# A graph layer on one core: half-block counts in PSUM, earlier loads in the head, and three blocks of the next chunk ahead of a fetch

## The chip, the cores and the metric

The kernel runs on one core of a Trainium2 chip. The metric is the time of one execution on the device, in microseconds (us), as a median over several executions. The profile shows one execution of the program with the busy times of five engines: TensorE (PE; its weight loads are PEld), VectorE (DVE), ScalarE (ACT), GpSimd (POOL) and SyncE (SP, which here only issues DMAs).

## The reference

The program computes one layer of a graph network. There are 12,500 nodes with 64 features each and 212,500 edges, sorted by their destination `dst`. For each edge, two rows of the normalised nodes and one edge weight go through a two-layer network with 128 hidden features; the results are summed per node `src`, which is not sorted; and a node network uses the sums.

```
h   = relu(layernorm(x))
e   = silu(concat(h[src], h[dst], edge_weight1) @ eW1 + eb1)
e   = silu(e @ eW2 + eb2)
agg = segment_sum(e, src)
out = x + silu(concat(h, agg) @ nW1 + nb1) @ nW2 + nb2
```

## The kernel before

**Tables.** The first matrix product is split. Table `ta` holds `h @ eW1` for the `src` half (three bf16 parts), table `tb` that for the `dst` half. `feed` is the generator that makes these tables from `x`, a few steps at a time, beside other work (`groups`, `products`, `normed`). A small table `tb0` for the first 2048 nodes is made at the very start (`first_rows`), so that the first `EARLY` blocks need not wait for `tb`.

**Buckets.** The 12,500 nodes are spread over `NB` = 100 buckets of 125. Edges are handled in the order given, in blocks of `BLK` = 1024, and each edge is sent to a row of its own in the DRAM array `q` of its bucket. There are 208 blocks, divided into 11 chunks: chunk 0 has 8 blocks, the ten others 20 (the last one slightly fewer). Each chunk has its own `q`.

**The sending side, per block s.**
- `load` (L256 on) issues on SP: the lists `bc` and `bb` of one block ahead (L265, L267), and two windows of the `tb` table, `win` (L277).
- `count` has three parts. First `pick` and `oh` (L302, L303), masks of which window row and which bucket an edge has; then the edge weights are loaded into `pick` (L288) and a scan counts each edge's place in its bucket (L306); then `own` keeps the count of the edge's own bucket (L314).

```
nc.vector.tensor_tensor_scan(
    run, oh, nil.to_broadcast([NB, BLK]), carry.get(c, -1.0), op0=OP.add, op1=OP.add
)
```

`run` (100 x 1024, fp32) lies in SBUF, and `nil`, one zero per partition, in the PSUM tile `misc`. `carry` is the last count of the block before.
- `send` has three parts: eight small matmuls write the places into `rank`, a part of `misc` (L333); sixteen matmuls give the row `qp` of each edge (L341), copied to `qs` (L348), and VectorE computes the destination `to` (L353); then GpSimd issues one indirect DMA for each 128 edges (L362), eight for a block. There are eight `qs` buffers of four such DMAs each, and four `to` buffers.

`send_all(c)` runs through the blocks of a chunk and yields after each part: `PIECES` = 3 pieces for a block, `send(s)` together with `count(s + 1)`. It also issues, on ACT's queue, the zero fills of the next chunk's `q`.

**The receiving side.** A chunk is processed in 25 batches of four buckets; a batch takes one step in chunk 0 and two in the others, 525 steps in all. `fetch` (L407, L412) loads a batch's `q` rows and `ta` rows on SP, `NQ` = 4 batches ahead. A step goes through `s_lr` (L430), `s_one_t` (L435), `s_pt` (L444, L451), `s_one` (L464), `s_p2` (L483), `s_seg` (sums per node into the PSUM tile `seg`, L497) and `s_add` (adds `seg` to `aggT` in SBUF, L508). In the last chunk each batch is followed by the node network (`nodes`).

**The order.** TensorE, VectorE, ScalarE and SyncE run in the order written by hand[...]. In the head, the lists are prepared and all of chunk 0 is sent, with four steps of `feed` after each piece. Then chunk 0's first four batches are fetched. From there the list `turn` gives the order within a step, with four hooks (`None`), at which pieces of the next chunk are sent and `feed` goes on:

```
turn = [
    (s_pt, 1), (s_add, -2), (s_one_t, 2), None, (s_bias, 1), (s_p2, 0), (s_one, 0), None, (s_seg, -1), None, (s_lr, 3), None,
]
```

How many pieces are due at a hook follows from `marks`: chunk c has to be sent completely before its first fetch is issued, and pieces are spread evenly between two such points.

[...] Before, `mm` takes four, `p2` two, `misc` one and `seg` one.

Of the kernel before, what the change touches and what calls it, by code (L numbers as in the profile page):

```python
# [28 lines left out]
F32 = mybir.dt.float32  # L29
# [4 lines left out]
OP = mybir.AluOpType  # L34
# [4 lines left out]
P = 128  # L39
L = 125  # L40
WL = 48
HB = 64
BLK = 1024
HALF = BLK // 2
TB = BLK // P
PAIR = 2 * BLK
G = 4
# [12 lines left out]
def tile_gnn(ctx: ExitStack, tc: tile.TileContext, x, src, dst, ew, eW1, eb1, eW2, eb2, nW1, nb1, nW2, nb2, out):  # L60
    nc = tc.nc
# [43 lines left out]
            dma(to[part], of[part])  # L105

    CH = 12
    NE, EARLY = 16, 24
    x_rows = x.rearrange("(l b) d -> l b d", b=NB)

    ident = const.tile([P, P], F32, name="ident")
# [127 lines left out]
    with ExitStack() as work:  # L239
# [5 lines left out]
                engines={mybir.EngineType.PE, mybir.EngineType.DVE, mybir.EngineType.Activation, mybir.EngineType.SP}  # L245
            )
        )
        misc = sgp.tile([P, 4 * TB], F32, name="misc")
        nc.vector.memset(misc[:, 2 * TB : 2 * TB + 1], 0.0)
        nil = misc[:NB, 2 * TB : 2 * TB + 1]  # L250
        oh = cnt.tile([NB, BLK], F16, name="oh")
        run = cnt.tile([NB, BLK], F32, name="run")
        carry = {}
        blk = {}
        nblocks = -(-E // BLK)
        chunk_of = [c for c, ch in enumerate(chunks) for _ in range(2 * (ch[1] - ch[0]))][:nblocks]  # L256

        def load(s, ahead=0):

            if s + ahead < nblocks:  # L260
                p, g = (s + ahead) // 2, (s + ahead) % 2
# [6 lines left out]
                blk[s + ahead] = [bc, bb]  # L268
            if 0 <= s < nblocks:
# [26 lines left out]
        def count(s):  # L296

            if s >= nblocks:
                return
            c = chunk_of[s]  # L300
            bc, bb, win, pick = blk[s]
            nc.vector.tensor_scalar(pick, bc, same, plus, op0=OP.is_equal, op1=OP.add)  # L302
            nc.vector.tensor_scalar(oh, bb[:NB, :], part[:NB, :], None, op0=OP.is_equal)  # L303
            yield
            weights(s)
            nc.vector.tensor_tensor_scan(  # L306
                run, oh, nil.to_broadcast([NB, BLK]), carry.get(c, -1.0), op0=OP.add, op1=OP.add
            )
            yield
            n = min(BLK, E - s * BLK)  # L310
            end = run[:, n - 1 : n]
            carry[c] = end
            own = wk.tile([NB, BLK], F16, name="own")
            nc.vector.tensor_tensor(own, run, oh, op=OP.mult)  # L314
            blk[s].append(own)
            if s + 1 == nblocks or chunk_of[s + 1] != c:
                u = wk.tile([NB, 1], F32, name="u")
                for limit, op in ((chunks[c][2] * P - 1, OP.is_gt), (chunks[c][3] - 1, OP.is_lt)):
                    nc.vector.tensor_scalar(u, end, float(limit), None, op0=op)
                    nc.vector.tensor_tensor(bad[:NB, 1:2], bad[:NB, 1:2], u, op=OP.add)  # L320
            yield

        def send(s):

            p, g = s // 2, s % 2
            c = chunk_of[s]
            _, _, cap, _, q = chunks[c]
            _, _, win, pick, run = blk.pop(s)
            n = min(BLK, E - s * BLK)
            nt = -(-n // P)  # L330
            rank = misc[:, (s % 2) * TB : (s % 2 + 1) * TB]
            for t in range(nt):
                nc.tensor.matmul(rank[:, t : t + 1], run[:, t * P : (t + 1) * P], fours[:NB, :], start=True, stop=True)  # L333
            yield

            qps = [mm.tile([P, G, H], F32, name="qp", tag="mm") for _ in range(2)]
            for t in range(G):
                for a in range(2):
                    half = slice(a * HB, a * HB + WL + 2)
                    if a * G + t < nt:  # L340
                        nc.tensor.matmul(  # L341
                            qps[a][:, t, :], pick[half, t * P : (t + 1) * P], win[half, :], start=True, stop=True
                        )
            halves = []
            for t0 in range(0, nt, G):
                qs = qsp.tile([P, G, W], F32, name="qs")
                m = min(G, nt - t0)
                nc.scalar.copy(qs[:, :m, :H], qps[t0 // G][:, :m, :])  # L348
                halves.append((t0, m, qs))
            for t0, m, qs in halves:  # L350
                if t0 == 0:
                    to = top.tile([P, TB], I32, name="to")
                    nc.vector.scalar_tensor_tensor(  # L353
                        to[:, :nt], rank[:, :nt], float(G * cap * P), bkE[:, g * TB : g * TB + nt, p], op0=OP.min, op1=OP.add
                    )
                at = g * TB + t0
                nc.scalar.copy(
                    qs[:, :m, H:], locE[:, at : at + m, p][:, :, None].to_broadcast([P, m, W - H])
                )
                for t in range(t0, t0 + m):  # L360
                    k = min(P, n - t * P)
                    i = nc.gpsimd.indirect_dma_start(  # L362
                        out=q[:],
                        out_offset=bass.IndirectOffsetOnAxis(ap=to[:k, t : t + 1], axis=0),
                        in_=qs[:k, t - t0, :],
                        in_offset=None,
                    )

                    tc.declare_no_dep(i.ins, group=f"rows{c}", reason="each edge has a row of its own")
                    tc.add_to_no_dep_group(f"rows{c}", i.ins)  # L370
                yield

        def send_all(c):
# [2 lines left out]
            zeros_left = list(fill(c + 1, nc.scalar, 7)) if c + 1 < len(chunks) else []  # L376
            each = -(-len(zeros_left) // len(mine))
            for s in mine:
                load(s + 2, 1)
                for f in zeros_left[:each]:  # L380
                    f()
                del zeros_left[:each]
# [14 lines left out]
        def fetch(i):  # L397
# [17 lines left out]
            batch[c, B] = [qt, a3, None]  # L415
            if c == len(chunks) - 1:
                node_in[B] = nodes_in(B, ndp[0])

# [3 lines left out]
            return batch[c, B], [((g * G + t) % n * G + (g * G + t) // n, (g * G + t) // n) for t in range(G)]  # L422

        def s_lr(k):
            (qt, _, _), tiles = of(k)
# [11 lines left out]

        def s_pt(k):

            (qt, a3, _), tiles = of(k)  # L440
# [15 lines left out]
            st[k]["e1"] = e1  # L456

        def s_one(k):
            (qt, _, _), tiles = of(k)
# [29 lines left out]

        def s_seg(k):  # L490
            c, B, n, g = steps[k]
            item, tiles = of(k)
            if g == 0:
                item[2] = sgp.tile([P, G, L], F32, name="seg")
            e2, one = st[k].pop("e2"), st[k].pop("one")
            for t, (j, b) in enumerate(tiles):
                nc.tensor.matmul(item[2][:, b, :], e2[:, t, :], one[:, t, :], start=j < G, stop=j >= G * (n - 1))  # L497

        def s_add(k):
            c, B, n, g = steps[k]  # L500
            if g < n - 1:
                return
            v = aggT[:, B * G : B * G + G, :]
            seg = batch.pop((c, B))[2]
            if c == 0:
                nc.vector.tensor_copy(v, seg)  # L506
            else:
# [192 lines left out]
        with tc.tile_pool(name="lists", bufs=1, side="right") as lp:  # L700
# [18 lines left out]
            for _ in turns(steps_, 3):  # L719
                if zero_fills:  # L720
                    zero_fills.pop(0)()
            for _ in turns([by_edges(sf, bkE)] + [first_rows(g) for g in range(0, NE, G)], 3):
                pass
            scale(0)
            load(-1, 1)
            load(0, 1)
            load(1, 1)
            for _ in by_edges(t, locE):
                pass
            for _ in count(0):  # L730
# [13 lines left out]
            nc.scalar.copy(b2f, p2)  # L744
        ld2 = work.enter_context(tc.tile_pool(name="ld2", bufs=NQ))
        ndp = []
        for i in range(NQ):
            fetch(i)


        first = -3
        marks, total = [(0, 0)], 0
        for c in range(1, len(chunks)):
            start = c * (NB // G) - NQ
            by = sum(x[2] for x in batches[: start + 1]) - 2
            total += PIECES * pending[c]
            marks.append((hooks * (by - first), total))
        pieces = itertools.chain.from_iterable(send_all(c) for c in range(1, len(chunks)))
        at = done = 0
        for k in range(first, len(steps) + 2):  # L760
            for s in turn:
                if s is None:
# [170 lines left out]
```

## Time and profile before

| | |
|---|---|
| median of 3 runs | 2703.32 us (2700.62 to 2704.18) |
| profiled execution: time | 2702.45 us |
| profiled execution: span | 2700.7 us |
| TensorE busy | 2188.2 us (81%) |
| VectorE busy | 1874.6 us (69%) |
| ScalarE busy | 1251.1 us (46%) |
| GpSimd busy | 1818.5 us (67%) |
| indirect DMAs (L362) | 1661, mean 1072 ns |
| scans (L306) | 208, mean 2341 ns (2278 in the 11 without a carry) |
| own (L314) | 208, mean 1220 ns |

A row of the profile names the line, the engine, the operation, and what it writes and reads; "idle before" is the time for which the engine did nothing just ahead of an instruction, with what released it. "issue" stands for time in which the engine waited for nothing that the profile shows. In the strip of slices each digit is the busy share of a fortieth of the span, in tenths.

### The profile page before, as it was taken

How to read it: one execution, taken by the hardware profiler on the slowest of the kernel's cores; microseconds unless marked ns; L12 is line 12 of the kernel's file. 1: busy time of each engine (PE TensorE's matmuls, PEld its weight loads, DVE VectorE, ACT ScalarE, POOL GpSimd, SP SyncE). 2: the span in 40 equal slices, each digit the busy share in tenths (PEclk: the TensorE clock that was granted, in tenths of full speed). 3: DMA queues.
4: the chain of work that ended last, by engine and by line, in shares of the span. 5: the costliest groups of instructions: out<-in, count | busy, mean ns of one | idle time of the engine just before them, and what ended most of it. 6: DMA issues, size and time to landing. Idle time of an engine off the chain costs nothing.

```text
span 2700.7 us, 59194 instructions
## 1 busy us (share of the span) xinstructions
PE 2188.2 (81%) x21814; PEld 2043.3 (76%) x21814; DVE 1874.6 (69%) x2634; ACT 1251.1 (46%) x2689; POOL 1818.5 (67%) x1728
## 2 busy tenths in 40 slices
PE   2436674898699599699879969959959987997997
PEld 1326574897699599599779869959958986996996
DVE  4736683796588488588768858848857885883443
ACT  2325551454355255355445535525535544553443
POOL 2546787777777777777777777777777777773000
PEclk9757786998899799799989989979989998998999
DMA  8668675876776777686787777767767755764441
GB/s 201 190 186 243 202 246 163 260 234 196 231 234 229 213 248 236 203 251 231 212 256 230 237 218 233 238 205 253 231 202 250 240 183 198 234 199 158 158 164 52
DMA packets 257969, 577.18 MB, mean 214 GB/s; under 512 B 51201, under 2 KB 110579, under 8 KB 257468
## 3 DMA queue, kind: packets, MB, share of 16 engines
q1 hardware_dynamic: 185096, 384.91, 44.3%
q0 software_dynamic: 54144, 123.04, 12.6%
q10 hardware_dynamic: 18434, 65.37, 10.5%
q8 instruction: 175, 2.87, 0.4%
q14 instruction: 120, 0.98, 0.1%
HBM read 361.44 MB, written 211.67 MB: 212 GB/s over the span
## 4 chain that ended last, share of the span: by engine, by line
PE 63%; DMA 13%; issue 6%; POOL 5%; DVE 2%; ACT 1%; SPq 0%; DVEq 0%; POOLq 0%; ACTq 0%
PE p L483 15%; PE seg L497 15%; PE pt L451 11%; DMA q<-qs,to 8%; PE pt L444 8%; PE qp L341 7%; POOL q L362 5%; PE lr L430 4%; DMA pick<-in_edge_weight_dram 3%; PE misc L333 1%; DMA bb<-rows 1%; PE z L216 1%; PE o L225 1%; DVE oneT L435 1%; PE z L219 1%
## 5 line engine op out<-in xcount | busy, mean ns | idle before, releaser
L362 POOL DMA_INDIRECT q<-qs,to x1661 | 1780.4, 1072 | 632.2 <-issue 445.6
L455 ACT ACTIVATE e<-pt 128x512 f32<-128x512 f32 x525 | 313.9, 598 | 778.0 <-PE pt L451 765.1
L483 PE MATMUL p<-w,e 128*128 128x128 f32 x4200 | 588.2, 284 | 2.2 <-ACT p L477 2.2
L497 PE MATMUL seg<-one,e 128*128 128x125 f32 x4200 | 576.8, 281 | 8.9 <-DVE aggT L506 5.7
L483 PEld LDWEIGHTS p<-w,e 128*128 128x128 f32 x4200 | 529.5, 198 | 27.5 <-issue 10.4
L497 PEld LDWEIGHTS seg<-one,e 128*128 128x128 f32 x4200 | 524.8, 196 | 11.2 <-ACT p L477 4.1
L435 DVE TENSOR_SCALAR oneT<-lr,part 125x512 bf16<-125x512 f32 x525 | 392.6, 748 | 197.5 <-PE lr L430 194.6
L306 DVE TENSOR_TENSOR_SCAN run<-oh,run,misc 100x1024 f32<-100x1024 f16 x197 | 461.1, 2341 | 1.0 <-PE misc L333 0.7
L451 PE MATMUL pt<-oneT,a 125*128 125x256 bf16 (+1 forms) x3300 | 444.6, 274 | 0.0
L341 PE MATMUL qp<-win,pick 50*128 50x128 f32 x3322 | 264.6, 300 | 205.0 <-DMA pick<-in_edge_weight_dram 119.9
L348 ACT COPY qs<-qp 128x512 f32<-128x512 f32 x416 | 224.7, 588 | 444.3 <-PE qp L341 312.0
L341 PEld LDWEIGHTS qp<-win,pick 50*128 50x128 f32 x3322 | 224.1, 202 | 237.8 <-issue 208.2
L444 PE MATMUL pt<-ident,qt 128*128 128x128 f32 x2100 | 332.8, 282 | 68.8 <-DVE oneT L435 68.8
L508 DVE TENSOR_TENSOR aggT<-aggT,seg 128x500 f32<-128x500 f32 x250 | 168.3, 673 | 315.7 <-PE seg L497 313.3
L464 DVE TENSOR_TENSOR one<-nodes,qt 128x500 f32<-128x500 f32 x525 | 353.4, 673 | 0.5 <-PE seg L497 0.5
L451 PEld LDWEIGHTS <-a 125*128 125x128 bf16 x3300 | 320.5, 100 | 34.5
L487 ACT ACTIVATE e<-p 128x512 f32<-128x512 f32 x525 | 314.6, 599 | 12.3 <-PE p L483 11.6
L477 ACT COPY p<-b2f 128x512 f32<-128x512 f32 x525 | 312.3, 595 | 0.1
L444 PEld LDWEIGHTS pt<-ident,qt 128*128 128x128 f32 x2100 | 228.4, 145 | 74.9 <-DVE oneT L435 72.9
L430 PE MATMUL lr<-identb,qt 128*125 128x128 bf16 x2100 | 215.1, 226 | 63.1 <-DMA qt<-q 63.0
L314 DVE TENSOR_TENSOR own<-run,oh 100x1024 f16<-100x1024 f32 x208 | 253.7, 1220 | 0.0
L430 PEld LDWEIGHTS <-qt 128*125 128x125 bf16 x2100 | 187.8, 140 | 75.6 <-DMA qt<-q 63.7
(122 smaller groups left out, 1094.5 us busy)
## 6 DMA issues: line engine op xcount, KB each, us to landing
qt<-q SPq DMA_DIRECT2D x250, 576.0 KB
a<-ta SPq DMA_DIRECT2D x275, 384.0 KB
q<-zeros ACTq DMA_DIRECT2D x30, 1638.0 KB
bb<-rows SPq DMA_DIRECT2D x208, 224.0 KB
bc<-rows SPq DMA_DIRECT2D x208, 128.0 KB
q<-qs,to POOLq DMA_INDIRECT x1661
win<-tb SPq DMA_DIRECT2D x416, 24.0 KB
ta<-parts SPq DMA_DIRECT2D x25, 384.0 KB
```

The lines of the kernel that those rows point to most:

```text
L306: nc.vector.tensor_tensor_scan(run, oh, nil.to_broadcast([NB, BLK]), carry.get(c, -1.0), op0=OP.add, op1=OP.add)
L341: nc.tensor.matmul(qps[a][:, t, :], pick[half, t * P : (t + 1) * P], win[half, :], start=True, stop=True)
L362: i = nc.gpsimd.indirect_dma_start(out=q[:], out_offset=bass.IndirectOffsetOnAxis(ap=to[:k, t : t + 1], axis=0), in_=qs[:k, t - t0, :], in ...
L430: nc.tensor.matmul(lr[:L, t, :], loc[:, at : at + 1].to_broadcast([P, L]), identb, start=True, stop=True)
L435: nc.vector.tensor_scalar(oneT, st[k].pop("lr")[:L], part1[:L, :], None, op0=OP.is_equal)
L444: nc.tensor.matmul(pt[:, t, :], qt[:, j, :H], ident, is_transpose=True, start=t == 0, stop=False, skip_group_check=True)
L451: nc.tensor.matmul(pt[:, cols, :], a3[:L, b, i, :], oneT[:, cols, :], start=False, stop=i == 2, skip_group_check=True)
L455: nc.scalar.activation(e1, pt, AF.Silu)
L464: nc.vector.tensor_tensor(one.rearrange("p (b j) l -> p b j l", j=n), nodes1[:, None, None, :].to_broadcast(wide), loc[:, tiles[0][1] : ti ...
L483: nc.tensor.matmul(p2[:, t, :], e1[:, t, :], w2, start=False, stop=t == G - 1, skip_group_check=True)
L487: nc.scalar.activation(e2, p2, AF.Silu)
L497: nc.tensor.matmul(item[2][:, b, :], e2[:, t, :], one[:, t, :], start=j < G, stop=j >= G * (n - 1))
```

## The change

Three things change together.

The counts: `run` is now one PSUM tile of 512 columns, and a block is scanned in two halves, each followed by its half of `own`. The second half's scan starts from the last count of the first. The first half stands in the second part of `count`, the other one in the third. `nil` becomes a tile in SBUF. So that `run` has a bank, `seg` and `rank` now share the tile `misc`[...], and `rank` has one buffer instead of two.

The head: the lists of block 0 are loaded (`load_rows(0)`) before `first_rows` issues its stores to `tb0`, and `scale(0)`, four short VectorE instructions, runs inside that loop.

The chunks: after the head's sending of chunk 0, three blocks (`LEAD` = 9 pieces) of chunk 1 are sent, again with four steps of `feed` after each piece, and only then come the first fetches. `marks` keep this distance up to the last chunk but one. `EARLY` grows from 24 to 30 blocks.

```
-    NE, EARLY = 16, 24
+    NE, EARLY = 16, 30
...
-        misc = sgp.tile([P, 4 * TB], F32, name="misc")
-        nc.vector.memset(misc[:, 2 * TB : 2 * TB + 1], 0.0)
-        nil = misc[:NB, 2 * TB : 2 * TB + 1]
+        misc = sgp.tile([P, G * L + TB], F32, name="misc")
+        seg = misc[:, : G * L].rearrange("p (b l) -> p b l", l=L)
+        rank = misc[:, G * L :]
+        run = sgp.tile([NB, HALF], F32, name="run")
         oh = cnt.tile([NB, BLK], F16, name="oh")
-        run = cnt.tile([NB, BLK], F32, name="run")
+        nil = cnt.tile([NB, 1], F32, name="nil")
+        nc.vector.memset(nil, 0.0)
...
-            nc.vector.tensor_tensor_scan(
-                run, oh, nil.to_broadcast([NB, BLK]), carry.get(c, -1.0), op0=OP.add, op1=OP.add
-            )
-            yield
-            n = min(BLK, E - s * BLK)
-            end = run[:, n - 1 : n]
-            carry[c] = end
             own = wk.tile([NB, BLK], F16, name="own")
-            nc.vector.tensor_tensor(own, run, oh, op=OP.mult)
             blk[s].append(own)
+            for h in range(2):
+                half = slice(h * HALF, (h + 1) * HALF)
+                n = min(HALF, E - s * BLK - h * HALF)
+                if n <= 0:
+                    break
+                nc.vector.tensor_tensor_scan(
+                    run, oh[:, half], nil.to_broadcast([NB, HALF]), carry.get(c, -1.0), op0=OP.add, op1=OP.add
+                )
+                end = carry[c] = run[:, n - 1 : n]
+                nc.vector.tensor_tensor(own[:, half], run, oh[:, half], op=OP.mult)
+                if h == 0:
+                    yield
...
-            rank = misc[:, (s % 2) * TB : (s % 2 + 1) * TB]
...
-            for _ in turns([by_edges(sf, bkE)] + [first_rows(g) for g in range(0, NE, G)], 3):
-                pass
-            scale(0)
-            load(-1, 1)
-            load(0, 1)
-            load(1, 1)
+            load_rows(0)
+            counting = count(0)
+            for i, _ in enumerate(turns([by_edges(sf, bkE)] + [first_rows(g) for g in range(0, NE, G)], 3)):
+                if i == 8:
+                    scale(0)
+            for i in range(2):
+                load(i)
...
+        LEAD = 3 * PIECES
+        for done in range(1, LEAD + 1):
+            next(pieces)
+            for _ in range(4):
+                next(feed, None)
         for i in range(NQ):
             fetch(i)
...
-        marks, total = [(0, 0)], 0
+        marks, total = [(0, LEAD)], 0
...
-            total += PIECES * pending[c]
-            marks.append((hooks * (by - first), total))
+            total += PIECES * chunk_of.count(c)
+            marks.append((hooks * (by - first), total + (LEAD if c + 1 < len(chunks) else 0)))
```

More of the change, by code (lines that the diff above doesn't have):

```diff
@@ L256, in tile_gnn, with load_rows @@
         chunk_of = [c for c, ch in enumerate(chunks) for _ in range(2 * (ch[1] - ch[0]))][:nblocks]
-        def load(s, ahead=0):
-            if s + ahead < nblocks:
-                p, g = (s + ahead) // 2, (s + ahead) % 2
+        def load_rows(s):
+            if s < nblocks:
+                p, g = s // 2, s % 2
                 r = rows[p, g]
@@ L267, in load @@
                 nc.sync.dma_start(bb[:112], bass.AP(tensor=r.tensor, offset=r.offset + BLK, ap=[[0, 112], [1, BLK]]))
-                blk[s + ahead] = [bc, bb]
-            if 0 <= s < nblocks:
+                blk[s] = [bc, bb]
+        def load(s):
+            load_rows(s + 1)
+            if s < nblocks:
                 p, g = s // 2, s % 2
@@ L378, in send_all @@
             for s in mine:
-                load(s + 2, 1)
+                load(s + 2)
                 for f in zeros_left[:each]:
@@ L414, in fetch @@
             )
-            batch[c, B] = [qt, a3, None]
+            batch[c, B] = [qt, a3]
             if c == len(chunks) - 1:
@@ L424, in s_lr @@
         def s_lr(k):
-            (qt, _, _), tiles = of(k)
+            (qt, _), tiles = of(k)
             loc = qt.rearrange("p j w -> p (j w)").bitcast(BF16)
@@ L438, in s_pt @@
         def s_pt(k):
-            (qt, a3, _), tiles = of(k)
+            (qt, a3), tiles = of(k)
             oneT = st[k].pop("oneT")
@@ L458, in s_one @@
         def s_one(k):
-            (qt, _, _), tiles = of(k)
+            (qt, _), tiles = of(k)
             c, B, n, g = steps[k]
@@ L491, in s_seg @@
             c, B, n, g = steps[k]
-            item, tiles = of(k)
-            if g == 0:
-                item[2] = sgp.tile([P, G, L], F32, name="seg")
+            _, tiles = of(k)
             e2, one = st[k].pop("e2"), st[k].pop("one")
             for t, (j, b) in enumerate(tiles):
-                nc.tensor.matmul(item[2][:, b, :], e2[:, t, :], one[:, t, :], start=j < G, stop=j >= G * (n - 1))
+                nc.tensor.matmul(seg[:, b, :], e2[:, t, :], one[:, t, :], start=j < G, stop=j >= G * (n - 1))
         def s_add(k):
@@ L503, in s_add @@
             v = aggT[:, B * G : B * G + G, :]
-            seg = batch.pop((c, B))[2]
+            del batch[c, B]
             if c == 0:
@@ L721, in tile_gnn @@
                     zero_fills.pop(0)()
-            for _ in turns([by_edges(sf, bkE)] + [first_rows(g) for g in range(0, NE, G)], 3):
-                pass
-            scale(0)
-            load(-1, 1)
-            load(0, 1)
-            load(1, 1)
+            load_rows(0)
[5 more added lines that the diff above has]
+                load(i)
             for _ in by_edges(t, locE):
                 pass
-            for _ in count(0):
+            for _ in counting:
                 pass
@@ L746, in tile_gnn @@
         ndp = []
+        pieces = itertools.chain.from_iterable(send_all(c) for c in range(1, len(chunks)))
+        LEAD = 3 * PIECES
[3 more added lines that the diff above has]
+                next(feed, None)
         for i in range(NQ):
@@ L755, in tile_gnn @@
             by = sum(x[2] for x in batches[: start + 1]) - 2
-            total += PIECES * pending[c]
-            marks.append((hooks * (by - first), total))
-        pieces = itertools.chain.from_iterable(send_all(c) for c in range(1, len(chunks)))
-        at = done = 0
+            total += PIECES * chunk_of.count(c)
+            marks.append((hooks * (by - first), total + (LEAD if c + 1 < len(chunks) else 0)))
+        at = 0
         for k in range(first, len(steps) + 2):
```

## The prediction, made before the result was known

> **What bounds the kernel now.** I start with the page's strip of 40 slices, because the share of busy time alone (TensorE 81%, GpSimd 67%) points at the wrong engine.
>
> ```profile
> PE   2436674898699599699879969959959987997997
> ...
> POOL 2546787777777777777777777777777777773000
> ```
>
> TensorE dips once per chunk, every 3.3 slices (221 us). GpSimd never dips: it holds one level from slice 4 until it has no more work, 250 us before the end. A level that never falls is either a limit or chance, so I look at single calls next, in the timeline from 1002 us.
>
> ```profile
> 1002.10 2.34 DVE L306 TENSOR_TENSOR_SCAN run<-oh,run,misc 100x1024 f32<-100x1024 f16 x1
> ...
> 1002.61 0.96 POOL L362 DMA_INDIRECT q<-qs,to  x1 [0.30 <-issue]
> ...
> 1003.88 0.97 POOL L362 DMA_INDIRECT q<-qs,to  x1 [0.30 <-issue]
> ...
> 1005.00 1.22 DVE L314 TENSOR_TENSOR own<-run,oh 100x1024 f16<-100x1024 f32 x1
> ...
> 1005.15 1.91 POOL L362 DMA_INDIRECT q<-qs,to  x1 [0.30 <-issue]
> ...
> 1007.37 1.66 POOL L362 DMA_INDIRECT q<-qs,to  x1 [0.30 <-issue]
> 1007.38 0.67 DVE L464 TENSOR_TENSOR one<-nodes,qt 128x500 f32<-128x500 f32 x1
> ```
>
> A free call takes 0.97 us and the next starts 0.30 us later: 1.27 us per scatter of 128 rows, however long the queue. A call that starts while VectorE runs own (L314) or one (L464) ends 0.84 us after that instruction's end instead. The scan (L306) delays none of the calls that start inside it. Counted over the trace, calls longer than 0.97 us cost 173.6 us: 76.0 for own (129 calls), 50.7 for one, 29.7 for pick and oh (L302, L303), 17 for others, and 0.3 for 377 calls that start inside a scan.
>
> GpSimd's line then adds up: first scatter at 67.7, 1661 calls x 1.272 = 2112.8, delays 173.6, gaps beyond 0.31 us 97.7, last scatter to end 248.5; together 2700.3 against a span of 2700.7. So **GpSimd's issue rate is the bound** from 68 to 2452 us; after that TensorE is (248.5 us for chunk 10's 50 steps). The windows say how much room TensorE has before that:
>
> ```profile
> 700.00:2450.00 1750.00, 1529.82 (x15836) 1448.71 (x15834) 1331.87 (x1821) 861.86 (x1841) 1339.96 (x1269) 0.94 0.71 225
> ...
> 1000.00:1050.00 50.00, 50.00 (x539) 47.47 (x538) 45.27 (x62) 28.40 (x61) 39.32 (x36) 1.00 0.72 234
> ```
>
> (busy us and count of PE, PEld, DVE, ACT, POOL, then clock.) At the 539 matmuls per 50 us of its full stretches the 15836 of these 1750 us need 1469 us; GpSimd's 1269 calls need 1614 without any delay. TensorE has some 280 us in hand there. The wait of SyncE's queue names the dips:
>
> ```profile
> SPq L407 <- DMA q<-qs,to: 350.2, 11, 34.7
> ```
>
> The first fetch of a chunk waits, 11 times and about 32 us each, until the last scatter of that chunk has landed. It runs in order, so loads of the next blocks (win L277, pick L288) stand behind it. GpSimd lives on its backlog meanwhile, with one exception and ten small ones: 26.5 us idle before the scatter at 202.15 us, and gaps of 1.7 to 4.5 us at the later boundaries (24.1 us in all).
>
> [...]own, one, L527 and L583 have two SBUF inputs and delay; the aggregation L508 (one input in PSUM) and the scan of before (second input in PSUM) do not. L536[...] delays too: its call at 156.69 us took 1.46 us and ended 0.84 after it. [...]
>
> **The change part by part.**
>
> *Counts.* 208 scans of 2341 ns become 416 of 512 elements. At 2.1 ns per element (twice the 1.05 between L464's 500 elements in 670 ns and L314's 1024 in 1220) and a fixed 0.19, a half takes about 1.27 us; a half of own about 0.69. A block costs VectorE 3.92 instead of 3.56 us, +75 us in all, beside GpSimd: VectorE was busy 1332 of those 1750 us.
> [...] own now reads run from PSUM: like L508 it should delay nothing, **-76.0 us**. But nil moves from PSUM to SBUF, so **each half scan now has two SBUF inputs**, oh and nil. A call that starts inside it is held to 0.13 us before its end: a window of 1.14 us, met by 1.14/1.27 = 0.90 of the halves, mean delay 0.57, so 0.51 us x 416 = 214 us. The same formula for own gives 1.09/1.27 x 0.545 x 208 = 97 where 76 was measured, a factor of 0.78; with it the scans cost 166. A held call often meets another such instruction behind the scan, so I take 195. Net **+119 us** (ends +90 and +138). [...]
>
> *One bank for rank and seg.* The order of the built program shows new waits: seg's matmuls wait for to (L353 of before) about once every other block, rank's matmuls for the aggregation, and the aggregation for rank. to itself waits, in VectorE's queue, for a scatter four blocks back, and one and oneT stand behind it as before; new is that TensorE's seg stands there directly, with p and pt behind it. No row prices it. Below: 0, since VectorE's stall stopped TensorE anyway. Above: 280 us of room over some 160 blocks is 1.7 us per block before it shows. I take 0, covered by GpSimd's queue; the tail has no rank.
>
> *Three blocks ahead.* 24 scatters of chunk 1, with their loads, go in SyncE's queue ahead of the four first fetches of chunk 0, and each later boundary finds three blocks already sent. The idle 26.5 us goes: chunk 0's 64 scatters took 108 us (67.7 to 175.6), 1.69 each, so 24 more end near 216, where before had done 11 of them. 13 scatters at 1.4 us are 18; with the whole gap it is 26. I take 24. The ten boundary gaps: the fetch then waits for at most 32 - 24 = 8 calls (backlog of 8 qs buffers of 4 calls, less the lead), and 24 calls stand queued, so 20 of 24.1 go. Of the starved stretch after 205 us (8.2, 4.9 and others, 24 us) I take 5, since 36 pieces of feed are done earlier. What is late next is GpSimd's own rate. Together **-49 us** (ends -15, -70). The zero fills and POOL's queue keep their counts; the tail keeps its 248.5, as chunk 10 gets no lead of an eleventh.
>
> *Lists ahead of stores.* The first scatter hangs on pick's weights (qp waits 7.19 us for them), which on SyncE stand behind the win loads, and these behind tb's four stores. Rows of block 0 now pass ahead of those stores; bc and bb take 1.1 us of issue and must wait for rows to land, so the stores start up to 3 us later, while a 3.0 us wait of bb goes. I take 0, between -3 and +3. nil's memset and EARLY cost nothing: the memset lies before x lands.
>
> Sum: 2702.45 (time of the profiled execution; 1.75 outside the span) + 119 - 49 + 0 = **2772 us**. The median of the runs shown is 2703.32, 0.9 more, which I leave.
>
> **The rivals.**
> 1. [...] Then -76 - 49: **2577 us**, faster. For it: no scan with nil in SBUF is in the trace. Against: L527 repeats mean and one repeats nodes, and both delay. It decides alone: break-even is a scan cost of 125 us, 0.30 us per half, below own's 0.365 per instruction.
> 2. [...] scans at 166 or less and all gaps gone (-70 or more) bring 2722; with a shorter half scan, about 2700, no change.
> 3. *The new bank wait bounds TensorE*: 2.5 us per block instead of 1.7 loses 0.8 x 208 = 166 us on top, **2940** with the scan, less if both overlap. For it: VectorE is 90% busy in full stretches, so to can be late. Against: the room above.
> 4. *The lead does not unblock the fetch*, if the backlog is longer than I count: 2772 + 20.
>
> **How the numbers follow.** [...] the sum as above 0.66 (own range 2722 to 2825); [...] lead pays for it 0.10 (half within 0.2%, half faster); [...] bank wait 0.04. Within 0.2%, 5 us, is about what a measurement of this kernel can tell from no change. Faster 0.25, same 0.05, slower 0.70. The range runs from 2570, through the middle of rival 1, to 2825.
>
> **What would show it.** Right: scatter calls that start inside a scan end 0.84 us after it, those inside own stay at 0.97, POOL's mean rises from 1072 to about 1144 ns, no gap near 176 to 202, SPq's wait for q falls from 350 to under 120 us, last scatter near 2523. Wrong: a POOL mean near 1030 (rival 1), or GpSimd gaps in mid span while seg waits on to (rival 3). A tail unlike 248 us would break the sum.

## The result: a little faster, and the profile after

The changed kernel takes 2695.37 us (median of 19 runs, 2686.15 to 2705.63) against 2702.63 for the kernel before (19 runs on the same chip): a ratio of 0.9972, 95% interval 0.996 to 0.9983, or 7 us less. The forecast was 2772 us. The profiled execution of after took 2686.15 us (span 2684.3), the shortest of its 19; the sums below are against that span. The 19 runs lie up to 19 us apart, so a few us between two profiled executions are not read as an effect.

GpSimd (POOL) still runs at one level until its work ends, with the same three empty slices behind it. The page's strip:

```profile
PE   2444786888998998799799889989889989997997
...
POOL 3564777777777777777777777777777777773000
```

GpSimd's line is split as in the prediction. A "delay" is what a scatter call takes beyond 0.967 us, a "gap" what passes between two calls beyond 0.305 us:

| | before | after | difference |
|---|---|---|---|
| first scatter | 67.7 | 63.3 | -4.4 |
| 1661 x 1.272 | 2112.8 | 2112.8 | 0 |
| delays | 174.2 | 187.2 | +13.0 |
| gaps | 98.3 | 74.2 | -24.1 |
| last scatter to end | 248.5 | 247.6 | -0.9 |
| span | 2700.7 | 2684.3 | -16.4 |

That these terms make up the span shows no bound: they do so by construction, in any kernel. They show where the time went, and the small gain is the balance of opposite terms. Each call is booked to the VectorE instruction that runs 0.15 us after its start, here and in all tables. So counted, the delays of own went from 76.3 to 0 us (184 calls now meet it and none is held), those of the scan from 0 to 128.3 (313 calls), those of `one` from 51.1 to 32.0, all others from 46.8 to 26.9. The groups of the page (busy us, mean ns; then idle before):

```profile
L371 POOL DMA_INDIRECT q<-qs,to x1661 | 1793.4, 1080 | 603.3 <-issue 415.4
...
L319 DVE TENSOR_TENSOR_SCAN run<-oh,run,nil 100x512 f32<-100x512 f16 x405 | 523.1, 1292 | 0.2
...
L323 DVE TENSOR_TENSOR own<-run,oh 100x512 f16<-100x512 f32 x416 | 287.7, 691 | 14.2
```

The mean of a call rose by 8 ns where 72 were forecast. Single calls show both the hold and what limits it. First, the timeline of VectorE from 1180 us:

```profile
1180.27 0.67 DVE L473 TENSOR_TENSOR one<-nodes,qt 128x500 f32<-128x500 f32 x1
1180.86 1.29 DVE L319 TENSOR_TENSOR_SCAN run<-oh,run,nil 100x512 f32<-100x512 f16 x1
...
1191.37 1.29 DVE L319 TENSOR_TENSOR_SCAN run<-oh,run,nil 100x512 f32<-100x512 f16 x1
...
1193.37 0.67 DVE L473 TENSOR_TENSOR one<-nodes,qt 128x500 f32<-128x500 f32 x1
1193.96 1.29 DVE L319 TENSOR_TENSOR_SCAN run<-oh,run,nil 100x512 f32<-100x512 f16 x1
```

and the calls of GpSimd beside it:

```profile
1181.39 1.52 POOL L371 DMA_INDIRECT q<-qs,to  x1 [0.30 <-ACT e L464]
...
1192.56 0.96 POOL L371 DMA_INDIRECT q<-qs,to  x1 [0.30 <-issue]
1193.83 1.05 POOL L371 DMA_INDIRECT q<-qs,to  x1 [0.31 <-DVE to L362]
1195.18 0.96 POOL L371 DMA_INDIRECT q<-qs,to  x1 [0.30 <-issue]
```

The call at 1181.39 starts inside a scan and ends 0.76 us after it: held, for 0.55 us. The call at 1193.83 starts inside `one` and ends 0.84 us after `one` (1194.04 to 1194.88). By then the next scan has begun; the next call comes at 1195.18, 0.07 us before that scan ends, and is free, as the call at 1192.56 was. **This scan, right behind `one`, delays no call of its own.** 277 of the 413 scans between the first and the last scatter stand directly behind `one`; how many of the scans are as cheap as this one is counted at e7.

SyncE's queue waits for the last scatter of a chunk a tenth as long as before (35.5 instead of 350.2 us):

```profile
SPq L416 <- DMA q<-qs,to: 35.5, 3, 30.9
```

and two waits around `to` have grown:

```profile
DVE to L362 <- DMA q<-qs,to: 198.1, 81, 9.4
...
PE misc L504 <- DVE to L362: 127.1, 51, 9.6
```

The first, VectorE waiting for scatters of an earlier block, goes with the lead: it is 75.6 us in before, 322.3 in e2 (the lead alone) and 69.4 in e13 (all but the lead). The second, seg's matmuls (tile misc) waiting until the instruction that makes `to` has read rank, needs the shared tile and the lead: it is 16.2 us in e13, and in e6, with rank in a tile of its own, it is not among the waits of 10 us or more.

### The profile page after: what moved, and what is told of

The parts are those of the page before. It is cut to its first block, busy times and chain, and to the rows that moved or that the text cites. A ratio compares the mean times of both kernels' runs of the same rounds, so it can differ in the third digit from the quotient of the medians.

```text
span 2684.3 us, 59579 instructions
## 1 busy us (share of the span) xinstructions
PE 2246.3 (84%) x21814; PEld 2083.4 (78%) x21814; DVE 1959.1 (73%) x3050; ACT 1249.9 (47%) x2687; POOL 1831.5 (68%) x1728
## 4 chain that ended last, share of the span: by engine, by line
PE 38%; DMA 28%; POOL 15%; issue 8%; DVE 6%; ACT 3%; SPq 2%; ACTq 0%; DVEq 0%; POOLq 0%
DMA q<-qs,to 18%; POOL q L371 15%; PE misc L504 9%; PE p L492 8%; PE pt L460 6%; PE pt L453 4%; DMA pick<-in_edge_weight_dram 4%; PE qp L350 4%; PE lr L439 2%; DMA xs<-in_x_dram 2%; DMA a<-ta 1%; DVE run L319 1%; DVE oneT L444 1%; ACT qs L357 1%; PE ab L180 1%
## 5 line engine op out<-in xcount | busy, mean ns | idle before, releaser
L371 POOL DMA_INDIRECT q<-qs,to x1661 | 1793.4, 1080 | 603.3 <-issue 415.4
L504 PE MATMUL misc<-one,e 128*128 128x125 f32 x4200 | 595.9, 287 | 155.5 <-DVE to L362 127.1
L504 PEld LDWEIGHTS misc<-one,e 128*128 128x128 f32 x4200 | 535.9, 200 | 171.0 <-issue 130.3
L319 DVE TENSOR_TENSOR_SCAN run<-oh,run,nil 100x512 f32<-100x512 f16 x405 | 523.1, 1292 | 0.2
L460 PE MATMUL pt<-oneT,a 125*128 125x256 bf16 (+1 forms) x3300 | 454.7, 278 | 0.0
L357 ACT COPY qs<-qp 128x512 f32<-128x512 f32 x416 | 230.5, 587 | 389.8 <-PE qp L350 212.7
L453 PE MATMUL pt<-ident,qt 128*128 128x128 f32 x2100 | 341.0, 287 | 30.6 <-DVE oneT L444 29.1
L496 ACT ACTIVATE e<-p 128x512 f32<-128x512 f32 x525 | 313.9, 598 | 16.4 <-PE p L492 15.8
L323 DVE TENSOR_TENSOR own<-run,oh 100x512 f16<-100x512 f32 x416 | 287.7, 691 | 14.2
L515 DVE TENSOR_TENSOR aggT<-aggT,misc 128x500 f32<-128x500 f32 x250 | 167.6, 670 | 149.7 <-PE misc L504 111.2
L453 PEld LDWEIGHTS pt<-ident,qt 128*128 128x128 f32 x2100 | 234.8, 148 | 36.4 <-DVE oneT L444 32.3
```

Source lines behind the costliest of these rows:

```text
L319: nc.vector.tensor_tensor_scan(run, oh[:, half], nil.to_broadcast([NB, HALF]), carry.get(c, -1.0), op0=OP.add, op1=OP.add)
L371: i = nc.gpsimd.indirect_dma_start(out=q[:], out_offset=bass.IndirectOffsetOnAxis(ap=to[:k, t : t + 1], axis=0), in_=qs[:k, t - t0, :], in ...
L453: nc.tensor.matmul(pt[:, t, :], qt[:, j, :H], ident, is_transpose=True, start=t == 0, stop=False, skip_group_check=True)
L460: nc.tensor.matmul(pt[:, cols, :], a3[:L, b, i, :], oneT[:, cols, :], start=False, stop=i == 2, skip_group_check=True)
L496: nc.scalar.activation(e2, p2, AF.Silu)
L504: nc.tensor.matmul(seg[:, b, :], e2[:, t, :], one[:, t, :], start=j < G, stop=j >= G * (n - 1))
```

## The experiments

Theory after the result: the half scan holds calls as forecast, but shares its delay where it stands behind another holder; the lead closes gaps; the bank costs nothing. Rivals: the scan hardly holds a call, and the delays come from elsewhere; or the scan's term is full-sized and the lead made up for it.

All runs together, with the ratio to the kernel before on the same chip, and delays and gaps (us) from the profiled execution of each. The kernel before took 2701.86 us beside e1 to e4, 2701.94 beside e5 to e8 and 2703.35 beside e13 to e16, so medians of different groups are compared as they stand.

| run | median us | ratio (95%) | delays | of these scan / own / `one` | gaps |
|---|---|---|---|---|---|
| before | 2702.63 | 1 | 174 | 0 / 76 / 51 | 98 |
| after | 2695.37 | 0.9972 (0.996 to 0.9983) | 187 | 128 / 0 / 32 | 74 |
| e1 nil in misc | 2672.92 | 0.989 (0.9869 to 0.9912) | 82 | 0 / 4 / 56 | 156 |
| e2 lead alone | 2705.99 | 1.0013 (1.0001 to 1.0024) | 198 | 1 / 92 / 72 | 72 |
| e3 counts alone | 2718.57 | 1.0059 (1.0037 to 1.008) | 194 | 132 / 0 / 33 | 98 |
| e4 head alone | 2699.6 | 0.9994 (0.9983 to 1.0005) | 169 | 0 / 70 / 54 | 102 |
| e5 nil in a bank of PSUM with rank | 2621.12 | 0.9704 (0.9682 to 0.9727) | 88 | 1 / 6 / 51 | 105 |
| e6 as e5, nil in SBUF | 2712.1 | 1.0036 (1.0024 to 1.0047) | 195 | 132 / 0 / 40 | 92 |
| e7 `one` behind the hooks | 2774.9 | 1.025 (1.0216 to 1.0283) | 273 | 164 / 1 / 29 | 81 |
| e8 thirds, nil in run's bank | 2629.49 | 0.9723 (0.9702 to 0.9744) | 98 | 1 / 3 / 71 | 109 |
| e13 after without lead | 2716.51 | 1.0056 (1.0039 to 1.0072) | 191 | 125 / 0 / 37 | 101 |
| e14 e5 without lead | 2633.17 | 0.9747 (0.973 to 0.9764) | 95 | 2 / 4 / 61 | 111 |
| e15 e8, node numbers in PSUM | 2576.96 | 0.9532 (0.9516 to 0.9548) | 31 | 0 / 1 / 2 | 124 |
| e16 e15, mm with three banks | 2563.29 | 0.9484 (0.9469 to 0.9499) | 35 | 0 / 3 / 5 | 112 |

**e1: nil in PSUM again**, as a column of misc, the rest as after.

```
-        misc = sgp.tile([P, G * L + TB], F32, name="misc")
+        misc = sgp.tile([P, G * L + TB + 1], F32, name="misc")
...
-        rank = misc[:, G * L :]
+        rank = misc[:, G * L : G * L + TB]
+        nil = misc[:NB, G * L + TB :]
...
-        nil = cnt.tile([NB, 1], F32, name="nil")
```

> The changed kernel with one edit: nil becomes column 508 of the PSUM tile misc, so the half scans have one SBUF input and one PSUM input. Theory A (GpSimd's issue rate is the bound[...]): the 127.6 us of delay of scatter calls that start inside a scan go to under 5 us, GpSimd's mean call falls from 1080 to about 1005 ns, and the time falls by about as much, to 2560 to 2620 us. Theory B (the delays are hidden, because TensorE with its boundary and bank waits is the bound): the delays go, but the time stays within 15 us of 2695, and GpSimd shows gaps in their place. A new cost for both: nil shares the bank of seg and rank, so scans now wait for matmuls of seg (a few tenths of a us each).

The scans still take 1290 ns, and 339 calls that start inside them lose 0.3 us instead of 128.3. So the hold comes from nil's place alone, and the rival "the scan hardly holds a call" is out. The time, 2672.92 us, lies between the two that were expected: of the 105 us less in delays, 82 come back as gaps. nil now shares a bank with seg, and in e5 and e8, where it does not, the gaps are 105 and 109 instead of 156. The waits of e1:

```profile
DVE run L319 <- PE misc L504: 180.6, 176, 6.7
...
PE misc L504 <- DVE run L319: 102.8, 67, 2.2
```

VectorE and TensorE wait for each other although they touch different columns of misc: the scans 176 times, 1.03 us on average, and seg's matmuls 67 times, 1.53 us, where a few tenths of a us for a scan were expected.

**e2, e3, e4: one part each** on the kernel before. e2 takes LEAD, marks and EARLY; e3 the counts with their banks; e4 the head's order.

> The kernel before with only the three blocks ahead (LEAD, marks, EARLY 30). Theory A: [...] (delays near 174 us), the gaps at boundaries and the 26.5 us gap go in part; 24 us less gaps, time 2670 to 2685. If the lead is worth the 49 us of the prediction: about 2655. Theory B (the fetch waits are the bound): over 60 us faster. Rival C (the lead is worth nothing by itself, since GpSimd is only shifted): 2700.

> The kernel before with only the counts in PSUM by halves, seg and rank in one bank, nil in SBUF. Theory A with back-to-back instructions sharing a delay: scan delays 120 to 135 us, none for own, net of all delays +10 to +20 us, time 2705 to 2725. If each half pays on its own as in the prediction: delays about 290, time about 2820. If the bank wait of seg on to costs time: above 2725 with GpSimd gaps that before does not have.

> The kernel before with only the lists of block 0 loaded ahead of the stores to tb0 and scale(0) inside that loop. Theory A: the first scatter moves from 67.7 to about 63 us and the time falls by 3 to 5 us, to about 2698. Rival: the head is bound by later waits, and the time stays at 2702.

e2: the gaps fall by 26 us, and the delays rise by 24 (own +16, `one` +21, others less). So it is not faster, against the 2670 to 2685 expected: the lead's gain was given back in held calls. e3: slower by 16.7, with 132 us for the scans, again far below the forecast's 195. e4: the first scatter comes at 63.1 instead of 67.7 us, and the median is 2.3 lower, with an interval that includes no change. The three parts add up to +18.5 us, and together they give -7.3.

**e5 and e6: a bank taken from mm** for rank (and, in e5, nil), so that seg has misc to itself. mm has three buffers instead of four, and the tile aux takes the place of the fourth.

```
-        mm = work.enter_context(tc.tile_pool(name="mm", bufs=4, space=PSUM))
+        mm = work.enter_context(tc.tile_pool(name="mm", bufs=3, space=PSUM))
...
-        misc = sgp.tile([P, G * L + TB], F32, name="misc")
+        misc = sgp.tile([P, G * L], F32, name="misc")
+        aux = sgp.tile([P, TB + 1], F32, name="aux")
...
+        rank = aux[:, :TB]
+        nil = aux[:NB, TB :]      # e5; in e6 nil stays in SBUF
```

> The changed kernel with three mm banks instead of four; the bank that comes free holds rank and nil, seg has its bank alone, so neither seg nor the scan waits for the other's bank. Theory A (e1's gaps of 156 us came from scans and seg waiting for each other in one bank): delays stay near 82 us, gaps fall to 75 to 100 us, time 2590 to 2625. Rival (the gaps come from TensorE being the next bound, whatever the banks): gaps stay near 150 and the time near 2670. A loss common to e5 and e6 is the price of three mm banks.

> The control of e5: the same three mm banks and the same banks for seg and rank, but nil stays in SBUF. Theory A: delays near 187 us as in the changed kernel, waits of seg on to (127 us) gone, yet the time within 15 us of 2695, since GpSimd is the bound. If the bank wait of seg had cost the change time: 2670 or less.

e5 against e6 is nil's place and nothing else: 91 us, of which 107 in the delays, less 13 in the gaps. e6 against after is two things at once, seg and rank in separate banks and one bank less for mm: the wait of seg on `to` is gone, and the kernel is 17 us slower (2712.1, just outside the range expected). So that wait of 127.1 us was hidden, or mm's fourth bank was worth more than it cost; e6 does not separate the two. The rows of the calls in e5, then in e6:

```profile
L372 POOL DMA_INDIRECT q<-qs,to x1661 | 1694.2, 1020 | 634.5 <-issue 416.1
```

```profile
L372 POOL DMA_INDIRECT q<-qs,to x1661 | 1800.8, 1084 | 621.1 <-issue 406.4
```

**e7: the scans moved away from `one`.** The order of after, with `one` behind the last hook; a scan then mostly follows oneT, which reads its matrix from PSUM and holds no call: in after 281 calls meet it and lose nothing.

```
-  (s_bias, 1), (s_p2, 0), (s_one, 0), None, (s_seg, -1), None, (s_lr, 3), None,
+  (s_bias, 1), (s_p2, 0), None, (s_seg, -1), None, (s_lr, 3), None, (s_one, 0),
```

> The changed kernel with s_one moved behind the last hook of a step[...]. Theory A (an instruction [...] right behind another costs almost nothing, since the call that the first one held is just being served): the scans' delay rises from 0.31 to 0.38 or more us per half (160 us or more), and one, now 0.7 us behind a scan, keeps at least its 32 us; all delays 215 to 250 us, time 2715 to 2750. Rival (each such instruction meets the calls by chance, and 0.31 is just the mean): delays stay at 187 and the time at 2695.

The same instructions in another order cost 80 us more, above the range expected, and GpSimd's gaps stay (81). The delays are 273 instead of 187, and this is the row:

```profile
L371 POOL DMA_INDIRECT q<-qs,to x1661 | 1879.0, 1131 | 609.0 <-issue 418.5
```

The 86 us are mostly of two kinds. The scans cost 35 us more (164), as expected. In after, a scan whose last scatter call had not been held delays the next call by 396 ns on average (303 scans); one whose last call had just been held, by 31 ns (110 scans). In e7 only 43 of 413 scans find the last call just held, and the others cost 388 ns. The price of an independent meeting is the same in both; what differs is how many are independent. A held call is not enough by itself: the 43 in e7 cost some 0.46 us each. Mostly oneT or another instruction stands there between the holder and the scan, and the next call then comes in the middle of the scan (14 scans behind oneT cost 0.52 us each, 13 behind `to` 0.73). The cheap place is the one directly behind the holder: in after 105 scans directly behind a `one` that had just held a call delay no call at all.

The other 49 us are the opposite of sharing. Calls that meet oh lose 60 us in e7 and 11 in after. In e7 `one` often stands directly behind oh, and 69 calls that start in oh (3 in after) are held through both, 0.82 us each. The two of VectorE, and the call:

```profile
1034.79 0.48 DVE L309 TENSOR_SCALAR oh<-bb,part 100x1024 f16<-100x1024 bf16 x1
1035.19 0.67 DVE L473 TENSOR_TENSOR one<-nodes,qt 128x500 f32<-128x500 f32 x1
...
1034.91 1.80 POOL L371 DMA_INDIRECT q<-qs,to  x1 [0.30 <-DMA q<-qs,to]
```

The call ends at 1036.71, 0.85 us after the end of `one` and 1.44 after that of oh. So of two holders in a row the second sometimes takes the waiting call as well: in after 88 calls held by `one` got through ahead of the scan behind it, and behind oh they (69 calls in e7) did not get through ahead of `one`. Why the pairs differ is open.

**e8: a block in three parts**, so that nil has a column in run's own bank, which only VectorE uses, and mm keeps four banks.

```
+        runs = sgp.tile([NB, 343], F32, name="run")
+        nil = runs[:, 342:343]
...
+            for h, (h0, h1) in enumerate(((0, 342), (342, 683), (683, BLK))):
```

> The changed kernel with nil in PSUM without a bank shared with TensorE: run is 342 columns, a block is scanned in three parts, and nil is column 342 of run's own bank, which VectorE alone uses. Seg and rank share a bank as in the change. Theory A: [...] (delays near 82 us) and no scan waits for seg, so gaps 75 to 110 us and time 2590 to 2630, faster than both kernels; VectorE has about 0.3 us more work per block. Rival (TensorE with the waits of seg on to is the next bound): gaps above 140 us, time near 2670 as in e1.

2629.49: the scans hold almost no call (1 us) without a bank taken from mm. The time is 8 us above e5; what part of that the 207 more scans and 207 more of own have is open. What is left of the delays is mostly `one`, 71 us.

**e9 to e12: four kernels on a chip that behaves otherwise.** There the kernel before itself took 3395 us instead of 2702, and GpSimd waited for copies of TensorE's results, as the waits of e9 show:

```profile
POOL q L371 <- ACT qs L366: 737.6, 174, 29.7
```

> The changed kernel without the three blocks ahead (counts and head stay). Theory A (the parts interact through the delays: the lead costs 24 us of delay [...], and none where own reads PSUM): gaps back near 98 us, delays 180 to 195, time 2710 to 2720, so that the lead is worth 15 to 25 us here and minus 4 alone. Rival (the parts add): the changed kernel plus 4 or less, about 2692 to 2700.

> e5 (three mm banks, nil and rank in a bank of their own) without the three blocks ahead. Almost no delays are left there that a lead could change. Theory A: delays stay near 88 us, gaps rise by 20 to 30 us over e5's 105, time 2640 to 2655. If the lead is worth the predicted 49 us: about 2670. If the lead is worth nothing [...]: 2621.

> e8 (thirds, nil in the bank of run) with the node numbers that s_one compares copied once into that bank too (125 columns), so that one has one SBUF input and one PSUM input. Theory A: one's delays (70.9 us in e8) go, all delays under 35 us, time 2560 to 2590 if GpSimd stays the bound. Rival (TensorE and its waits are nearly the bound by now): gaps grow by as much as delays fall, time 2610 to 2630.

> e11 with three mm banks and rank in the bank that comes free, so seg does not wait for to. Theory A: 5 to 15 us below e11, as e5 is 8 below e8. Rival (three mm banks hold TensorE up, which shows once GpSimd is faster): above e11.

e9 took 3391.45 (ratio 1.0002, 0.9971 to 1.0032), e10 3638.12 (1.07), e11 3664.2 (1.0781), e12 3680.1 (1.0831). The versions with fewer delays were the slower ones there. Since GpSimd was not the bound, these runs say nothing of the lead or of `one` in the regime of this case. TensorE was slower there (a matmul of seg took 305 ns on average in e9 and 282 in e13, at a granted clock of 0.85 and 0.90); whether that accounts for the 700 us is not settled. The same four kernels were run once more, as e13 to e16, beside a kernel before of 2703.35 us.

**e13 and e14: no lead**, in after and in e5 (first fetches ahead of chunk 1, the marks and EARLY of before).

```
-        LEAD = 3 * PIECES
-        for done in range(1, LEAD + 1):
-            next(pieces)
-            for _ in range(4):
-                next(feed, None)
...
-        marks, total = [(0, LEAD)], 0
+        marks, total = [(0, 0)], 0
```

> The change without its three blocks ahead (counts and head alone), beside a kernel before of about 2702 us. If the parts add up: 2700 + 16.7 - 2.3 = 2710 to 2720, and the three blocks ahead are then worth some 20 us to the scans in halves, where they were worth nothing to own. If the lead is worth nothing here either: 2692 to 2700. GpSimd's gaps beyond 0.305 us should be back at about 98 us (74 with the lead), the delays near 190.

> The version with nil in the freed PSUM bank (2621 us), without its three blocks ahead. If the lead closes gaps [...], 2640 to 2655 (gaps back by 24 us or more). If it is given back as on the kernel before, 2616 to 2626.

e13 is 2716.51: without the lead the parts do add up (2701.86 + 16.7 - 2.3 = 2716.3), and with scans in own's place the lead is worth some 21 us (2716.51 to 2695.37). It takes 26.5 us from the gaps, as in e2, and the delays stay (191 to 187). In e14 (2633.17, between the two ranges expected) it is worth 12 us, 6 of gaps and 7 of delays. So the lead's own effect on the gaps holds, and the odd one is e2, where own and `one` took 37 us more from the calls. Why the calls met own and `one` more often in e2 is open: no run separates it.

**e15 and e16: `one` without its hold**, on top of e8. The node numbers that `one` compares are copied once into free columns of run's bank, so that `one` has a single SBUF input; e16 takes a bank from mm for rank besides.

```
+        nodes_ps = runs[:, 343:468]
+        nc.vector.tensor_copy(nodes_ps, nodes1)
...
-                nodes1[:, None, None, :].to_broadcast(wide),
+                nodes_ps[:, None, None, :].to_broadcast(wide),
```

> The version in thirds (2629 us, delays 98 of which 71 to 'one') with the node numbers read from PSUM by 'one', so that it has one SBUF input. If GpSimd stays the bound: delays near 25, 2560 to 2590. If TensorE's side becomes the bound, or the shared bank of run and node numbers makes new waits: gaps rise by 40 us or more, and 2610 to 2640.

> The same with three banks for mm and rank in a bank of its own. If the wait between seg's and rank's matmuls costs something here, 5 to 15 us below the one before; if it is hidden, within 5 us of it or above it by what the fourth bank of mm was worth (0 to 10).

In e15 the 248 calls that meet `one` lose 2 us instead of 71, and 53 us are gained. The parts of e16's span are 62.9 + 2112.8 + 35.0 + 111.9 + 245.7 = 2568.3 against 2567.6. The row of e16:

```profile
L374 POOL DMA_INDIRECT q<-qs,to x1661 | 1641.2, 988 | 642.4 <-issue 394.5
```

A free call takes 0.967, so 21 ns per call is all the delay that is left. Giving mm's fourth bank to rank is worth 14 us here, of which 12 lie in the gaps; from after to e6 the same step cost 17 us, and why the two differ is open. **e16, 2563.29 us, is the fastest version: 5.2% below before, 4.9% below after.**

## Why the prediction was wrong, point by point

- **The bound: right, but not by the argument given.** The prediction reads it from the sum of GpSimd's line. That sum closes for any kernel; in e9, where GpSimd waits for others, it closes too (61.7 + 2112.8 + 186.3 + 776.7 + 251.8 = 3389.3 of 3388.5). What shows the bound is that the time follows the delays: from e6 to e5 they fall by 107 us and the time by 91, from e8 to e15 by 67 and 53, and from after to e7 they rise by 86 and 80.
- **"Each half scan now has two SBUF inputs", and so it holds calls: right**, shown by e1 (0.3 us lost in scans instead of 128.3) and by e5 against e6 (1 instead of 132). Rival 1, a half scan that holds no call, is refuted, though nil is one element per partition, repeated. The other cases that the prediction names, booked as above in before: 4 calls met L527 and lost 2.0 us, 15 met L583 and lost 7.2, 2 met L536 and lost 0.7; 62 met the aggregation L508 and lost nothing. On VectorE no cost of the hold is seen: a scan takes 1292 ns with nil in SBUF and 1290 with it in PSUM.
- **The size of the scans' term: the step that failed.** "I take 195", measured 128. The working had 0.51 x 0.78 = 0.40 us per half as the price of a meeting, and that is right where a scan meets the calls independently (0.396 in after, 0.388 in e7). But it was applied to all 416 halves, and 29 us were added because "a held call often meets another such instruction behind the scan". For a scan directly behind `one` the sign is reversed. A call released by `one` ends 0.84 us after it and the next starts 0.30 us later, 1.14 in all; the scan that began 0.08 us before `one`'s recorded end ends at 1.21, and the end of a scan delays no call: of 180 calls in after that start in the last 0.18 us of one, none loses over 0.01 us. So the next call mostly is not held. Of 413 scans, 110 came so and cost 31 ns. 303 x 0.396 + 110 x 0.031 = 123 of the 128. The order in VectorE's queue was in the built program: s_one stands directly ahead of a hook in turn. With the scans away from it, e7 measured 164 for them. That e7's time, 2774.9, comes near the forecast of 2772 is chance, as 49 us of its rise lie in oh.
- **The other delays: a second term that failed.** They were left unchanged at 98 us, without a reason, and measured 59: `one` 19 us less, and pick, oh, rows_a and parts 20 less. e3 has 62, so the fall comes with the counts. That of `one` lies in the calls that meet it ahead of pick (27 us before, 6 after), and not in those with a scan or own behind it (22 and 24); its cause is open. Together the counts' term was +119, and the delays rose by 13; e3 has +16.7 us for the counts alone.
- **"Three blocks ahead", -49: half of it came.** Gaps fell by 24. The later boundaries gave 16.5 of the 20 forecast. The starved stretch at the start was mis-sized: from 170 to 330 us the gaps went from 47.4 to 37.8, 10 us where 24 + 5 were taken. The gap of 26.5 us shrank, but GpSimd still ran out of work: its timeline has 12.91 us of idle at 221, waiting for a scan (L319), and 6.06 and 6.25 us at 183 and 232. That scan stood in VectorE's queue behind a step of feed, which waited 15.40 us for its load of x. What was late next was this, and not "GpSimd's own rate".

```profile
217.62 0.95 DVE L531 TENSOR_REDUCE mean<-xs 128x12 f32<-128x768 f32 x1 [15.40 <-DMA xs<-in_x_dram]
...
221.06 0.96 POOL L371 DMA_INDIRECT q<-qs,to  x1 [12.91 <-DVE run L319]
```

- **"Lists ahead of stores", 0 between -3 and +3**: the first scatter came 4.4 us earlier (4.6 in e4); that the time gains from it is not shown, as e4's 2.3 us are within its interval.
- **"One bank for rank and seg", 0: no cost seen.** The wait came (127.1 us, 51 times), and e6 does not isolate what it costs. Rival 3 with its 166 us is out: GpSimd's gaps are 74 us in all, 24 less than before. Besides that wait, after shows the aggregation waiting for rank's matmuls, which write other columns of misc (36.8 us, 34 times).
- **Rival 2** came nearest with "about 2700", but not by its way: it wanted all gaps gone (-70), and 24 went. With the scans at 128, own's 76 and these 24 gone, the sum would still be +28; the 39 us less in the other delays and some 5 us of the head and the tail made it -16. That it lands near no change is luck.
- **The sum:** against the profiled execution the forecast was 86 us too high: the scans 67, the other delays 39 and the head and tail 5 too high, the lead's gain 25 too large.
- **The signs**: SPq's wait for q at 35.5 us, under 120, right; calls inside own at 0.97 us, right; held calls inside a scan end 0.76 to 0.77 us after it where 0.84 was said; gaps of 6.06 and 2.91 us remain between 176 and 202 where none was said; the last scatter at 2436.6 for 2523, and the mean at 1080 for 1144, wrong with the terms above.

## What to carry to other kernels

When GpSimd issues indirect DMAs back to back, look in the trace for the VectorE instructions that hold its calls. Where one of them has two SBUF inputs and one of these is a small constant, keep a copy of it in PSUM: here copies of nil and of the node numbers took the delays from 187 to 31 us and the kernel to 2577 us (e15, which scans a block in thirds). Put such a constant into a PSUM tile that no other engine works in: in e1, with nil beside seg, scans and seg's matmuls waited for each other (180.6 and 102.8 us), and 82 of the 105 us came back as gaps. And price holders by their order in the queue, pair by pair: a scan directly behind `one` was nearly free after a held call (31 instead of 396 ns), and `one` directly behind oh held the same call a second time (0.82 us for each of 69 calls in e7).

## What had not been expected of the hardware

- A held call isn't released at the end of the VectorE instruction: it ends 0.84 us after `one` or own, and 0.76 to 0.77 after a scan, where a free call takes 0.97. If a held call still takes 0.97 us once it goes on, it goes on some 0.13 us (`one`, own) and 0.2 us (scan) before the recorded end; that is an estimate from these three figures.
- A call that starts close to the start of a scan mostly escapes it: of 72 calls in after that start between 0.10 us before and 0.09 us after a scan's recorded start, three were held through the scan, and all nine that start 0.10 to 0.15 us after it were. The call at 1191.29 us runs beside a scan from 1191.37 on and takes 0.96 us.
- Another chip ran the same kernel before in 3395 us instead of 2702, and in e9 there GpSimd waited 737.6 us for copies of TensorE's results; the versions that were faster here by less delay were 7 to 8% slower than before there.
